# Rows of adjacency and x mapped by halves, and the first two outer products run in turn

## The chip, the cores and the metric

The kernel runs on one core of one Trainium2 chip. The metric is the device time of one execution in microseconds (us), the median of several runs.

## The reference

Sixteen graphs `x` of 1024 nodes with 128 features share one adjacency matrix `adj` (1024 x 1024), everything in fp32. Two layers follow each other, each closed by a residual sum and a layernorm over the features:

```python
def _L0_gnn_ref(x, adj, weight, bias):
    support = jnp.einsum('bnf,fo->bno', x, weight)
    output = jnp.einsum('nm,bmo->bno', adj, support)
    return output + bias
...
x = _layernorm(x + _L0_gnn_ref(x, adj, L0_gnn_weight, L0_gnn_bias), axis=-1)
x = _layernorm(x + _L1_gnn_ref(x, adj, adj, ...), axis=-1)
```

The second layer is a gated recurrent update of five steps. Each step multiplies every graph by `adj` and then applies gates with small weights (`w3`, `w4`, `w5`, `u3`, `u5`). The same product "adjacency times features" is thus made once in layer 0 and five times in layer 1.

## The kernel before

**The product.** The graphs are taken four at a time (`QUAD`), in four groups `q`. The product of `adj` with a group is made by Strassen's scheme in Winograd's form, two levels deep: an outer product of 2 x 2 blocks is seven block products, numbered 1 to 7, and each of those is again made of seven. The left factors of the outer level are `outer[1]` to `outer[7]`: 1 and 2 are the upper blocks of the transposed adjacency, 4 and 7 the lower ones, and 5, 6, 3 are the sums `s1`, `s2`, `s4`. `left[n]` holds the seven inner left factors of outer product `n`: some are quarters of `outer[n]`, the others sums in the tiles `e`. The right factors are pieces of the rows and sums of them, in `inner` and `tsum`.

**A chain.** `chain` (L358) runs the seven inner products for one or two outer products at once, in the order 1, 5, 6, 2, 7, 3, 4. One inner product of one outer product is two matmuls of 128x256 (L398). Results go to three PSUM banks: `pa` for 1 and 2, `pc` for 5 and 3, `pb` for 6, 7 and 4. After 1, ScalarE copies `pa` to `pb` (L382), so 6 has to wait for that copy, and 2 reuses `pa`. After 7 and 3, VectorE adds the bank to a result that was copied out before (L386, L387); after 5, 6, 2 and 4 ScalarE copies the bank out. `aggregate` (L417) calls the chains in the order 12 (outer products 1 and 2 together), 3, 67, 54. `hooks` are functions called ahead of a named inner product, which puts their instructions there in program order.

**The start.** The adjacency arrives as eight blocks `c` of 128 rows, 512 KB each, four into `agg` and four into `hid`; `x0` and `x1` stand between them in the queues of SP and ACT, `x2` and `x3` at the end (L127 to L133). Row `p`, chunk `c` of a graph is its row `8p + c`. `turn_adj` (L181) transposes a block on TensorE in two groups of four 128x128 pieces, one for each half `j` of the columns, into banks from a ring of three; VectorE copies out half 0 of the first four blocks (L193) and ScalarE everything else (L195), into `blk` (the tile `a`). Ahead of the transposes stand twelve products of the identity with itself (L200). Then come `inner_left_12`, the inner left sums for outer products 1 and 2 in four instructions 128x1024 wide (L168 to L171), the sums of the rows (L317 to L320), and the first chain, 12.

In the first group, the hooks of chain 12 bring in ahead of 5: `turn_rest`, the transposes of the last four blocks with the two halves of `s1` (L701); `added_sums`, which negates rows on ScalarE (L684) into `tsum[2]` and `tsum[0]` and issues from POOL a transfer that adds `x` to each (L685); and `added_left`, which negates `outer[7]` on ScalarE (L669) and adds `outer[1]` to it by two more transfers from POOL (L671). Ahead of 6 come `outer_left`, which makes `s2` (L705) and `s4` (L706), 128x2048 wide each, and the inner left sums of 3, and the row sums of 3. Ahead of 7 come `rest_sums` (L688, L689) and the inner left sums of 6 and 7. POOL then loads the next group's rows (L733).

**Order.** Each engine runs its instructions in the order of the built program. A scheduler makes that order; `keep_in_program_order` holds an instruction to its place in the source, and `issue_after` puts instructions behind another.

**After the first group**, chains, projections by `w0` with their layernorm, and later the gated steps follow each other on TensorE. Rows between steps go through DRAM (`turned`, `closing`, `hidden`); layer 0's result is kept in `saved`. Results leave through SP (L281), the last ones partly through ScalarE's queue (L296).

Of the kernel before, what the change touches and what calls it, by code (L numbers as in the profile page):

```python
# [20 lines left out]
def kernel(  # L21
# [76 lines left out]
            turns[0] = (i + 1) % 3  # L98
        return ps_m.tile([P, HALF], F32, tag=f"g{i}", name=name)

    def as_rows(b, src):
        return src[b].rearrange("(p c) d -> p c d", c=C)

    def chunked(t):
        return t.rearrange("p (c d) -> p c d", c=C)
# [4 lines left out]

    def load(q, dst, src_of, ks=range(QUAD)):
        for k in ks:
            nc.sync.dma_start(dst[:, k], src_of(q * QUAD + k))

    def x_rows(b):
        return x[b].rearrange("(p c) d -> p (c d)", c=C)

    def saved_rows(b):
        return saved[b]


    queues = (nc.sync, nc.scalar)

    adj_rows = adj.rearrange("(h p n c) m -> n h p c m", h=2, n=4, c=2)
    raws = [agg[:, c] if c < CH else hid[:, c - CH] for c in range(C)]

    for i, c in enumerate([*range(CH), "x0", "x1", *range(CH, C), "x2", "x3"]):  # L127
        queue = queues[i % 2 if i < 6 else 0]
        if isinstance(c, str):
            k = int(c[1])  # L130
            queue.dma_start(rows[:, k], x_rows(k))
        else:
            queue.dma_start(raws[c], adj_rows[c // 2, c % 2])  # L133
# [43 lines left out]
    def inner_left_12():  # L177
        a = [[blk[0][:, :, 2 * j : 2 * j + 2, ts(i, QT)] for j in range(2)] for i in range(2)]
        return left_sums(*a[0], *a[1], e12[:, :, 0], e12[:, :, 1], e12[:, :, 3], e12[:, :, 2])

    def turn_adj(c):  # L181
        cols = raws[c].rearrange("p (q k) -> p k q", k=C)
        i, at = divmod(c, CH)
        for j in range(2):
            pt = bank(f"pt_adj_{c}_{j}")
            pt3 = pt.rearrange("p (k q) -> p k q", k=CH)
            for k in range(CH):
                op = nc.tensor.transpose(pt3[:, k, :], cols[:, j * CH + k, :], ident)
                if c < CH:
                    tc.keep_in_program_order(op)  # L190
            dst = blk[i][:, j, :, ts(at, P)]
            if j == 0 and i == 0:
                nc.vector.tensor_copy(dst, pt3)  # L193
            else:
                nc.scalar.copy(dst, pt3)  # L195


    for t in (pb, *seeded):
# [1 line left out]
            nc.tensor.matmul(t[:, ts(k, P)], ident, ident, start=(k == 0), stop=True,  # L200
                             skip_group_check=True)
    for c in range(CH):
        turn_adj(c)
    last_left = inner_left_12()


    w0_sb = const.tile([P, D], F32, name="w0_sb")
# [41 lines left out]
    def layernorm(y, tag, store, now=False):  # L249
# [28 lines left out]
            )  # L278

        def put():  # L280
            nc.sync.dma_start(store, y)  # L281

        if now == "DVE":
            def step():
                for c in range(n):
                    pin(nc.vector.tensor_scalar(
                        y[:, c, :], y[:, c, :], shift[:, c : c + 1], rstd[:, c : c + 1],
                        ALU.add, ALU.mult,
                    ))
                put()  # L290
            return step
        elif now is True:

            for c in range(n):
                pin(apply(c))
            pin(nc.scalar.dma_start(store, y))  # L296
# [24 lines left out]

    def blocks_of(src, ns):

        if ns in ((1, 2), (3,)):
            v = src.rearrange("p b (h j x) -> p b h j x", h=2, j=2)
            if ns == (1, 2):
                return lambda j, k: v[:, k, :, j]
            return lambda j, k: v[:, 2 + k, 1:2, j]
        at = {(6, 7): slice(1, 3), (5, 4): slice(0, 4, 3)}[ns]
        return lambda j, k: tsum[:, at, k, ts(j, QT)]  # L330

    def sums_of(src, ns, pinned=False):
        t = inner[0 if ns in ((1, 2), (6, 7)) else 1]
# [24 lines left out]
    def chain(tag, src, turned, ns, results, hooks, order=(1, 5, 6, 2, 7, 3, 4)):  # L358

        xs = blocks_of(src, ns)
        t = inner[0 if ns in ((1, 2), (6, 7)) else 1]
# [53 lines left out]
    def aggregate(tag, src, hooks, turned=True):  # L417
# [8 lines left out]
            v = t.rearrange("p o (k i n) -> p o k i n", k=2, i=2)  # L426
            return lambda i, k: v[:, :, k, i]

        chain(f"12_{tag}", src, turned, (1, 2), into(first), hooks.get(12, {}))
        if turned:  # L430
            sums_of(src, (3,), True)
            outer = outer_sums(src, True, False, True)
# [27 lines left out]
    def project(q, k, y):  # L460

        b = q * QUAD + k
        y = chunked(y)
        for h in range(2):
            po = seeded[h]
            po3 = po.rearrange("p (k d) -> p k d", k=CH)
            with tc.high_priority():
                tc.keep_in_program_order(
                    nc.scalar.copy(po3, b0_bc[:, None, :].broadcast_to([P, CH, D]))
                )  # L470
            for c in range(CH):
# [6 lines left out]
        layernorm(y, f"0_{b}", chunked(saved[b]))  # L478

# [160 lines left out]
    def finish(q, k, y):  # L640
        for h in range(2):
            finish_half(q, k, h, chunked(y))

    def normalize(q, k, y, now=False):
        b = q * QUAD + k
        layernorm(chunked(y), f"1_{b}", as_rows(b, out), now)

    def normalize_part(q, k, cols, y, now):
        b = q * QUAD + k
        return layernorm(  # L650
            chunked(y)[:, cols], f"1_{b}_{cols.start}", as_rows(b, out)[:, cols], now
        )

    def call(f, *args):
        return lambda: f(*args)
# [2 lines left out]
    def projections(q):  # L658

        room = rooms[q % 2]  # L660
        ys = [ypad[0], ypad[1], room[:, 2], room[:, 3]]
        for k in (2, 3):
            nc.sync.dma_start(ys[k], x_rows(q * QUAD + k))
        return {a: [call(project, q, k, ys[k])] for k, a in enumerate((5, 2, 3, "end"))}

    def added_left():
# [7 lines left out]
    def added_sums():  # L674


        v = [
            x[2 * i : 2 * i + 2].rearrange("b (p c) d -> p b (c d)", c=C)[:, :, ts(j, HALF)]
            for j in range(2) for i in range(2)
        ]  # L680
        (lo, hi), ((lo0, hi0), (lo1, hi1)) = (rows[:, 0:2], rows[:, 2:4]), (v[:2], v[2:])
        put = tc.keep_in_program_order
        for i, negative, rest in ((2, hi[:, :, :HALF], hi1), (0, lo[:, :, :HALF], hi0)):
            put(nc.scalar.mul(tsum[:, i], negative, -1.0))  # L684
            put(nc.gpsimd.dma_start(tsum[:, i], rest, accum_op=ALU.add))  # L685
# [4 lines left out]

    rooms = [rows, hid]

    def turn_rest():
        for c in range(CH, C):
            turn_adj(c)
            if c % 2:
                outer_s1(c // 2 - 2)

    def outer_s1(at):
        cols = ts(at, QT)  # L700
        nc.vector.tensor_add(s1[:, :, cols], outer[7][:, :, cols], outer[4][:, :, cols])  # L701

    def outer_left():
        put = tc.keep_in_program_order
        nc.vector.tensor_sub(s2, s1, outer[1])  # L705
        put(nc.vector.tensor_sub(s4, outer[2], s2))  # L706
        inner_left(3)

    for q in range(NQ):
        room = rooms[q % 2]  # L710
        hooks = {}
        if q == 0:
            hooks[12] = {
                5: [turn_rest, added_sums, added_left],
                6: [outer_left, call(sums_of, rows, (3,))],
                7: [rest_sums, call(inner_left, 6), call(inner_left, 7)],
            }
            hooks[67] = {1: [call(inner_left, 5), call(inner_left, 4)]}
# [7 lines left out]
        def fetch(q=q):  # L726
            drain(99, 0)
            if q == 0:

                for dst, b in [(hid[:, k], QUAD + k) for k in range(QUAD)] + [  # L730
                    (ypad[k], k) for k in range(2)
                ]:
                    tc.keep_in_program_order(nc.gpsimd.dma_start(dst, x_rows(b)))  # L733
                load_layer1_weights()
                return
            for k in range(2):
                nc.sync.dma_start(ypad[k], x_rows(q * QUAD + k))
            if q + 1 < NQ:
                load(q + 1, rooms[(q + 1) % 2], x_rows)
            else:  # L740
# [11 lines left out]
        if q == 0:  # L752
            with tc.issue_after(last_left.ins):
                aggregate(f"x{q}", room, hooks, False)
        else:
            aggregate(f"x{q}", room, hooks, False)

# [3 lines left out]

    def close_load(q, k):
        fetch_rows(k, None, closing[k], ypad[0])
        tc.keep_in_program_order(nc.sync.dma_start(spare, saved_rows(q * QUAD + k)))

    def close(q, k):
        t = ypad[0].rearrange("p (n d c) -> p n c d", n=4, c=2)
        y = spare.rearrange("p (n c d) -> p n c d", n=4, c=2)  # L770
        tc.keep_in_program_order(nc.vector.tensor_add(y, y, t))
        strict[0] = True
        layernorm(chunked(spare), f"1_{q * QUAD + k}", as_rows(q * QUAD + k, out))
        strict[0], closed[0] = False, last_stats[0]

    def next_load(q, k):
        tc.keep_in_program_order(nc.sync.dma_start(spare, saved_rows(q * QUAD + k)))

    def next_turn(k):
        turn_hidden(k, spare, [ypad[1]])  # L780
# [175 lines left out]
```

## Time and profile before

| What | Value |
|---|---|
| median of 3 runs | 1771.18 us (1771.13 to 1771.88) |
| span of the profiled execution | 1769.3 us |
| what lies around the span, against the median | 1.9 us; the page gives no total of its own for the profiled execution |
| instructions | 19948 |
| HBM read and written | 93.98 MB and 65.01 MB |

The span runs from the first to the last instruction of the profiled execution; the runs are timed from outside, so a little more lies around it. "PE" is TensorE's matmuls, "PEld" its weight loads, "DVE" VectorE, "ACT" ScalarE, "POOL" GpSimd, "SP" SyncE; a "q" behind a name is that engine's queue of DMA issues. In a line of the timeline the first number is the start in us from the span's start, the second the duration, and the bracket at the end is the idle time before it and who ended it. The landing of a transfer is counted from its issue; the blocks of the adjacency took 4.0 to 10.3 us, the two transfers of L685 6.9 and 8.4 us, and the two of L671 9.0 and 10.6 us.

### The profile page before, as it was taken

What the parts mean: (1) busy time and instruction counts of PE and PEld (TensorE: products, weight loads), DVE (VectorE), ACT (ScalarE), POOL (GpSimd) and SP (SyncE); (2) the same over time, 40 slices, a digit from 0 to 9 for tenths busy, and PEclk for the clock granted to TensorE, in tenths of its full rate; (3) what the DMA queues carried; (4) which work ended last, traced back from release to release, by engine and by line L of the source; (5) the groups of instructions that cost most, each with busy time, mean ns of one, the idle gap of its engine ahead of it and who ended that gap; (6) DMA issues with size and microseconds to landing.
All of it is one profiled execution on the core that took longest, in us unless ns stands there. A gap on an engine that the chain in (4) does not pass through costs nothing.

```text
span 1769.3 us, 19948 instructions
## 1 busy us (share of the span) xinstructions
PE 1757.7 (99%) x6709; PEld 1264.5 (71%) x6709; DVE 1302.9 (74%) x2286; ACT 799.2 (45%) x1424; POOL 103.6 (6%) x152
## 2 busy tenths in 40 slices
PE   9999999999999999999999999999999999999997
PEld 8888885766758577685867758586675857668584
DVE  7977777676766857777777667777778577777778
ACT  4355555344352434435354442535445353443537
POOL 1202120000000000000000000000000000000004
PEclk9999999999999999999999999999999999999999
DMA  8144354141422505143351424324243241514232
GB/s 276 49 143 143 120 130 107 26 114 30 96 60 72 143 13 130 48 121 68 87 131 54 114 54 101 81 75 119 53 114 98 58 92 28 131 25 107 60 84 95
DMA packets 405332, 161.34 MB, mean 91 GB/s; under 512 B 388336, under 2 KB 389488, under 8 KB 405232
## 3 DMA queue, kind: packets, MB, share of 16 engines
q1 hardware_dynamic: 402960, 153.01, 34.1%
q0 software_dynamic: 1696, 5.24, 1.1%
q10 hardware_dynamic: 576, 1.84, 0.3%
q8 instruction: 53, 0.87, 0.2%
q14 instruction: 47, 0.39, 0.1%
HBM read 93.98 MB, written 65.01 MB: 90 GB/s over the span
## 4 chain that ended last, share of the span: by engine, by line
PE 98%; DMA 1%; DVE 0%; POOL 0%; ACT 0%; issue 0%; POOLq 0%; SPq 0%; DVEq 0%; ACTq 0%
PE pb L398 25%; PE pc L398 14%; PE pa L398 14%; PE pu L516 8%; PE ph L539 8%; PE ph L540 8%; PE pu L498 8%; PE seeded L531 8%; PE pc_x L398 3%; PE pa_x L398 3%; PE seeded L472 2%; DMA hid<-in_adj_dram 1%; DMA agg<-in_adj_dram 0%; PE pt L630 0%; PE pt_end L831 0%; POOL rstd L265 0%
## 5 line engine op out<-in xcount | busy, mean ns | idle before, releaser
L398 PE MATMUL pb<-e,inner 128*128 128x256 f32 x864 | 206.3, 379 | 0.2 <-ACT pb L382 0.2
L555 DVE TENSOR_TENSOR tsum<-tsum,hid 128x512 f32<-128x512 f32 x158 | 108.7, 688 | 106.4 <-ACT tsum L550 106.3
L550 ACT ACTIVATE tsum<-ph,bh 128x512 f32<-128x512 f32 x158 | 108.6, 687 | 164.3 <-PE ph L540 164.2
L398 PEld LDWEIGHTS pb<-e,inner 128*128 128x128 f32 x864 | 167.7, 194 | 19.5 <-ACT pb L382 0.9
L516 PE MATMUL pu<-agg,w_t 128*128 128x512 f32 x320 | 163.7, 593 | 0.0
L539 PE MATMUL ph<-agg,w_t 128*128 128x512 f32 x320 | 163.4, 592 | 0.0
L531 PE MATMUL seeded<-agg,w_t 128*128 128x512 f32 x320 | 163.4, 592 | 0.0
L540 PE MATMUL ph<-tsum,u_t 128*128 128x512 f32 x320 | 163.4, 592 | 0.0
L498 PE MATMUL pu<-hid,u_t 128*128 128x512 f32 x320 | 157.0, 592 | 0.0
L519 ACT ACTIVATE tsum<-pu,br 128x512 f32<-128x512 f32 x160 | 110.1, 688 | 85.5 <-PE pu L516 85.5
L398 PE MATMUL pb<-s,inner 128*128 128x256 f32 x576 | 148.4, 380 | 0.0
L398 PE MATMUL pb<-a,inner 128*128 128x256 f32 x576 | 143.9, 379 | 0.0
L526 DVE TENSOR_TENSOR tsum<-tsum,hid 128x512 f32<-128x512 f32 x160 | 110.2, 688 | 37.7 <-ACT tsum L519 37.7
L398 PE MATMUL pc<-e,inner 128*128 128x256 f32 x560 | 134.3, 379 | 0.0
L398 PEld LDWEIGHTS pb<-s,inner 128*128 128x128 f32 x576 | 110.5, 194 | 24.6 <-issue 10.2
L534 ACT ACTIVATE tsum<-seeded,bz 128x512 f32<-128x512 f32 x160 | 110.0, 688 | 29.3 <-PE seeded L531 29.3
L398 PEld LDWEIGHTS pb<-a,inner 128*128 128x128 f32 x576 | 111.9, 194 | 12.4
L398 PEld LDWEIGHTS pc<-e,inner 128*128 128x128 f32 x560 | 109.1, 195 | 12.7 <-issue 0.7
L540 PEld LDWEIGHTS ph<-tsum,u_t 128*128 128x128 f32 x320 | 60.8, 190 | 76.5 <-issue 59.1
L539 PEld LDWEIGHTS ph<-agg,w_t 128*128 128x128 f32 x320 | 60.6, 190 | 75.1 <-issue 74.4
L498 PEld LDWEIGHTS pu<-hid,u_t 128*128 128x128 f32 x320 | 60.8, 190 | 73.5 <-issue 72.2
L556 DVE TENSOR_TENSOR tsum<-tsum 128x512 f32<-128x512 f32 x158 | 109.1, 691 | 4.9
(192 smaller groups left out, 2856.3 us busy)
## 6 DMA issues: line engine op xcount, KB each, us to landing
turned<-ypad SPq DMA_DIRECT2D x48, 512.0 KB, 3.8
rows<-turned SPq DMA_DIRECT2D x192, 128.0 KB, 2.8
hvs<-saved SPq DMA_DIRECT2D x24, 512.0 KB, 4.1
rows<-saved SPq DMA_DIRECT2D x20, 512.0 KB, 3.8
hid<-hidden SPq DMA_DIRECT2D x64, 128.0 KB, 3.3
turned<-ypad SPq DMA_DIRECT2D x32, 256.0 KB, 2.9
rows<-turned SPq DMA_DIRECT2D x128, 64.0 KB, 2.1
hidden<-ypad SPq DMA_DIRECT2D x12, 512.0 KB, 4.1
```

The lines of the kernel that those rows point to most:

```text
L398: product = nc.tensor.matmul(bank_of[a][:, ts(o, QT)], chunk(a, o, c), left[n][a][:, c, :], start=(a in (1, 5) and o == 0 and c == 0), sto ...
L498: in_order(nc.tensor.matmul(pu, w_t["u3"], hid[:, k, ts(h, HALF)], start=True, stop=True, skip_group_check=True))
L516: in_order(nc.tensor.matmul(pu, w_t["w4"], agg[:, k, cols], start=False, stop=True, skip_group_check=True))
L519: pin(nc.scalar.activation(rh[:, cols], pu, AF.Sigmoid, bias=br))
L526: pin(nc.vector.tensor_mul(rh[:, cols], rh[:, cols], hid[:, k, cols]))
L531: in_order(nc.tensor.matmul(pz, w_t["w3"], agg[:, k, cols], start=False, stop=True, skip_group_check=True))
L534: pin(nc.scalar.activation(z_of[k % 2][:, cols], pz, AF.Sigmoid, bias=bz))
L539: in_order(nc.tensor.matmul(ph, w_t["w5"], agg[:, k, cols], start=True, stop=False))
L540: in_order(nc.tensor.matmul(ph, w_t["u5"], rh_of[k % 2][:, cols], start=False, stop=True))
L550: pin(nc.scalar.activation(hv, ph, AF.Tanh, bias=bh))
L555: pinned(nc.vector.tensor_sub(hv, hv, hid[:, k, cols]))
L556: pinned(nc.vector.tensor_mul(hv, hv, z_of[k % 2][:, cols]))
```

## The change

Row `p`, chunk `c` of a graph is now row `512h + 4p + c`, with `h` the half: a half of the chunks is a half of the graph's rows. The adjacency's rows follow the same rule, so that the left half of the columns of the first four blocks, with the first halves of `x0` and `x1`, holds all that outer product 1 needs. These come first, as 256 KB pieces on both queues; the second halves follow on SP, then the last four blocks, then `x2` and `x3`. ScalarE makes all copies of the transposes, and all transposes keep their program order.

In the first group, outer products 1 and 2 run as two chains one after the other. `inner_left_12` goes; `start_sums(n)` makes the inner left sums and the row sums of one outer product, in turn, 128x512 and 128x256 wide. The second halves of the first four blocks are transposed ahead of inner product 2 of chain 1, the last four blocks ahead of inner product 1 of chain 2. The other groups keep chain 12.

Stores to `out` are split in two where they hold all eight chunks; loads of `x` carry two runs of 2 KB for a partition instead of one of 4 KB.

```diff
-        return src[b].rearrange("(p c) d -> p c d", c=C)
+    def as_rows(b, src, h):
+        return src[b, ts(h, HALF)].rearrange("(p c) d -> p c d", c=CH)
...
-        return x[b].rearrange("(p c) d -> p (c d)", c=C)
+        return x[b].rearrange("(h p c) d -> p h (c d)", h=2, c=CH)
...
-    adj_rows = adj.rearrange("(h p n c) m -> n h p c m", h=2, n=4, c=2)
+    adj_rows = adj.rearrange("(i h p n c) m -> i n h p c m", i=2, h=2, n=2, c=2)
...
-    for i, c in enumerate([*range(CH), "x0", "x1", *range(CH, C), "x2", "x3"]):
...
+    for j in range(2):
+        for c in range(CH):
+            load_adj(queues[c % 2 if j == 0 else 0], c, ts(j, HALF))
+        for k in range(2):
+            load_x(queues[k if j == 0 else 0], k, j)
+    for c in range(CH, C):
+        load_adj(nc.sync, c)
+    for k in (2, 3):
+        nc.sync.dma_start(by_half(rows[:, k]), x_rows(k))
...
-            if j == 0 and i == 0:
-                nc.vector.tensor_copy(dst, pt3)
-            else:
-                nc.scalar.copy(dst, pt3)
+            nc.scalar.copy(blk[i][:, j, :, ts(at, P)], pt3)
...
-        turn_adj(c)
-    last_left = inner_left_12()
+        turn_adj(c, (0,))
...
-        chain(f"12_{tag}", src, turned, (1, 2), into(first), hooks.get(12, {}))
+        if 1 in hooks:
+            for n in (1, 2):
+                chain(f"{n}_{tag}", src, turned, (n,), into(first[:, n - 1 : n]), hooks[n])
+        else:
+            chain(f"12_{tag}", src, turned, (1, 2), into(first), hooks.get(12, {}))
...
+    def start_sums(n):
+
+        lt = left[n]
+        pairs = [
+            lambda: nc.vector.tensor_add(lt[5], quarter(n, 1, 0), lt[4]),
+            lambda: nc.vector.tensor_sub(lt[6], lt[5], lt[1]),
+            lambda: nc.vector.tensor_sub(lt[7], lt[1], quarter(n, 1, 0)),
+            lambda: nc.vector.tensor_sub(lt[3], lt[2], lt[6]),
+        ]
+        right = inner_sums(
+            blocks_of(rows, (n,)), [sums_for((n,))[:, i] for i in range(4)]
+        )
+        for f in pairs:
+            tc.keep_in_program_order(f())
+            tc.keep_in_program_order(next(right))
+
+    def turn_first_rest():
+        for c in range(CH):
+            turn_adj(c, (1,))
+        start_sums(2)
...
-        nc.vector.tensor_sub(s2, s1, outer[1])
+        put(nc.vector.tensor_sub(s2, s1, outer[1]))
+        sums_of(rows, (3,), True)
         put(nc.vector.tensor_sub(s4, outer[2], s2))
...
-            hooks[12] = {
-                5: [turn_rest, added_sums, added_left],
-                6: [outer_left, call(sums_of, rows, (3,))],
+            hooks[1] = {2: [turn_first_rest]}
+            hooks[2] = {
+                1: [turn_rest],
+                5: [added_sums],
+                6: [added_left, outer_left],
                 7: [rest_sums, call(inner_left, 6), call(inner_left, 7)],
             }
...
-            with tc.issue_after(last_left.ins):
-                sums_of(rows, (1, 2))
+            start_sums(1)
```

More of the change, by code (lines that the diff above doesn't have):

```diff
@@ L99, in bank @@
         return ps_m.tile([P, HALF], F32, tag=f"g{i}", name=name)
-    def as_rows(b, src):
-        return src[b].rearrange("(p c) d -> p c d", c=C)
+    def as_rows(b, src, h):
+        return src[b, ts(h, HALF)].rearrange("(p c) d -> p c d", c=CH)
     def chunked(t):
@@ L112, in load, with by_half, load_adj, load_x @@
         for k in ks:
-            nc.sync.dma_start(dst[:, k], src_of(q * QUAD + k))
+            nc.sync.dma_start(by_half(dst[:, k]), src_of(q * QUAD + k))
+    def by_half(t):
+        return t.rearrange("p (h y) -> p h y", h=2)
     def x_rows(b):
-        return x[b].rearrange("(p c) d -> p (c d)", c=C)
+        return x[b].rearrange("(h p c) d -> p h (c d)", h=2, c=CH)
     def saved_rows(b):
-        return saved[b]
+        return by_half(saved[b])
     queues = (nc.sync, nc.scalar)
-    adj_rows = adj.rearrange("(h p n c) m -> n h p c m", h=2, n=4, c=2)
+    adj_rows = adj.rearrange("(i h p n c) m -> i n h p c m", i=2, h=2, n=2, c=2)
     raws = [agg[:, c] if c < CH else hid[:, c - CH] for c in range(C)]
-    for i, c in enumerate([*range(CH), "x0", "x1", *range(CH, C), "x2", "x3"]):
[L128 to L131, printed above, removed]
-        else:
-            queue.dma_start(raws[c], adj_rows[c // 2, c % 2])
+    def load_adj(queue, c, cols=slice(None)):
+        queue.dma_start(raws[c][:, cols], adj_rows[c // 4, c // 2 % 2, c % 2][:, :, cols])
+    def load_x(queue, k, h):
+        queue.dma_start(rows[:, k, ts(h, HALF)], x_rows(k)[:, h])
+    for j in range(2):
[7 more added lines that the diff above has]
+        nc.sync.dma_start(by_half(rows[:, k]), x_rows(k))
     power = const.tile([P, C], F32, name="power")
@@ L175, in inner_left, with turn_adj @@
         left_sums(lt[1], lt[2], quarter(n, 1, 0), lt[4], lt[5], lt[6], lt[7], lt[3], *put)
[L177 to L182, printed above, removed]
+    def turn_adj(c, js=(0, 1)):
+        cols = raws[c].rearrange("p (j q k) -> p j k q", j=2, k=CH)
         i, at = divmod(c, CH)
-        for j in range(2):
+        for j in js:
             pt = bank(f"pt_adj_{c}_{j}")
@@ L187, in turn_adj @@
             for k in range(CH):
[L188 to L191, printed above, removed]
-            if j == 0 and i == 0:
-                nc.vector.tensor_copy(dst, pt3)
-            else:
-                nc.scalar.copy(dst, pt3)
+                tc.keep_in_program_order(
+                    nc.tensor.transpose(pt3[:, k, :], cols[:, j, k, :], ident)
+                )
+            nc.scalar.copy(blk[i][:, j, :, ts(at, P)], pt3)
     for t in (pb, *seeded):
@@ L280, in put @@
         def put():
-            nc.sync.dma_start(store, y)
+            for dst, of in store:
+                nc.sync.dma_start(dst, y[:, of])
         if now == "DVE":
@@ L295, in layernorm @@
                 pin(apply(c))
-            pin(nc.scalar.dma_start(store, y))
+            for dst, of in store:
+                pin(nc.scalar.dma_start(dst, y[:, of]))
         else:
@@ L322, in blocks_of @@
     def blocks_of(src, ns):
-        if ns in ((1, 2), (3,)):
+        if ns in ((1, 2), (3,), (1,), (2,)):
             v = src.rearrange("p b (h j x) -> p b h j x", h=2, j=2)
@@ L327, in blocks_of @@
                 return lambda j, k: v[:, k, :, j]
+            if ns in ((1,), (2,)):
+                return lambda j, k: v[:, k, ns[0] - 1 : ns[0], j]
             return lambda j, k: v[:, 2 + k, 1:2, j]
@@ L330, in blocks_of, with sums_for @@
         return lambda j, k: tsum[:, at, k, ts(j, QT)]
+    def sums_for(ns):
+        if ns in ((1,), (2,)):
+            return inner[0][:, :, ns[0] - 1 : ns[0]]
+        return inner[0 if ns in ((1, 2), (6, 7)) else 1]
     def sums_of(src, ns, pinned=False):
-        t = inner[0 if ns in ((1, 2), (6, 7)) else 1]
+        t = sums_for(ns)
         for op in inner_sums(blocks_of(src, ns), [t[:, i, : len(ns)] for i in range(4)]):
@@ L362, in chain @@
         xs = blocks_of(src, ns)
-        t = inner[0 if ns in ((1, 2), (6, 7)) else 1]
+        t = sums_for(ns)
         w = len(ns) * QT
@@ L477, in project @@
                 nc.vector.tensor_add(y[:, ts(h, CH), :], po3, y[:, ts(h, CH), :])
-        layernorm(y, f"0_{b}", chunked(saved[b]))
+        layernorm(y, f"0_{b}", [(chunked(saved[b]), slice(None))])
     strict = [False]
@@ L642, in finish, with both_halves @@
             finish_half(q, k, h, chunked(y))
+    def both_halves(b):
+        return [(as_rows(b, out, h), ts(h, CH)) for h in range(2)]
     def normalize(q, k, y, now=False):
         b = q * QUAD + k
-        layernorm(chunked(y), f"1_{b}", as_rows(b, out), now)
+        layernorm(chunked(y), f"1_{b}", both_halves(b), now)
     def normalize_part(q, k, cols, y, now):
         b = q * QUAD + k
-        return layernorm(
-            chunked(y)[:, cols], f"1_{b}_{cols.start}", as_rows(b, out)[:, cols], now
-        )
+        h, at = divmod(cols.start, CH)
+        part = chunked(y)[:, cols]
+        store = as_rows(b, out, h)[:, at : at + part.shape[1]]
+        return layernorm(part, f"1_{b}_{cols.start}", [(store, slice(None))], now)
     def call(f, *args):
@@ L662, in projections @@
         for k in (2, 3):
-            nc.sync.dma_start(ys[k], x_rows(q * QUAD + k))
+            nc.sync.dma_start(by_half(ys[k]), x_rows(q * QUAD + k))
         return {a: [call(project, q, k, ys[k])] for k, a in enumerate((5, 2, 3, "end"))}
@@ L677, in added_sums @@
         v = [
-            x[2 * i : 2 * i + 2].rearrange("b (p c) d -> p b (c d)", c=C)[:, :, ts(j, HALF)]
+            x[2 * i : 2 * i + 2, ts(j, HALF)].rearrange("b (p c) d -> p b (c d)", c=CH)
             for j in range(2) for i in range(2)
@@ L691 @@
     rooms = [rows, hid]
+    def start_sums(n):
[8 more added lines that the diff above has]
+            blocks_of(rows, (n,)), [sums_for((n,))[:, i] for i in range(4)]
+        )
+        for f in pairs:
[5 more added lines that the diff above has]
+        start_sums(2)
     def turn_rest():
@@ L700, in outer_s1 @@
         cols = ts(at, QT)
-        nc.vector.tensor_add(s1[:, :, cols], outer[7][:, :, cols], outer[4][:, :, cols])
+        tc.keep_in_program_order(
+            nc.vector.tensor_add(s1[:, :, cols], outer[7][:, :, cols], outer[4][:, :, cols])
+        )
     def outer_left():
         put = tc.keep_in_program_order
-        nc.vector.tensor_sub(s2, s1, outer[1])
+        put(nc.vector.tensor_sub(s2, s1, outer[1]))
+        sums_of(rows, (3,), True)
         put(nc.vector.tensor_sub(s4, outer[2], s2))
@@ L732, in fetch @@
                 ]:
-                    tc.keep_in_program_order(nc.gpsimd.dma_start(dst, x_rows(b)))
+                    tc.keep_in_program_order(nc.gpsimd.dma_start(by_half(dst), x_rows(b)))
                 load_layer1_weights()
@@ L736, in fetch @@
             for k in range(2):
-                nc.sync.dma_start(ypad[k], x_rows(q * QUAD + k))
+                nc.sync.dma_start(by_half(ypad[k]), x_rows(q * QUAD + k))
             if q + 1 < NQ:
@@ L751 @@
             hooks[54][4] = [turn_weights]
[L752 to L756, printed above, removed]
+        aggregate(f"x{q}", room, hooks, False)
     spare = hvs.rearrange("p h x -> p (h x)")
@@ L765, in close_load @@
         fetch_rows(k, None, closing[k], ypad[0])
-        tc.keep_in_program_order(nc.sync.dma_start(spare, saved_rows(q * QUAD + k)))
+        tc.keep_in_program_order(nc.sync.dma_start(by_half(spare), saved_rows(q * QUAD + k)))
     def close(q, k):
@@ L772, in close @@
         strict[0] = True
-        layernorm(chunked(spare), f"1_{q * QUAD + k}", as_rows(q * QUAD + k, out))
+        layernorm(chunked(spare), f"1_{q * QUAD + k}", both_halves(q * QUAD + k))
         strict[0], closed[0] = False, last_stats[0]
     def next_load(q, k):
-        tc.keep_in_program_order(nc.sync.dma_start(spare, saved_rows(q * QUAD + k)))
+        tc.keep_in_program_order(nc.sync.dma_start(by_half(spare), saved_rows(q * QUAD + k)))
     def next_turn(k):
```

## The prediction

> **What bounds the kernel now.** I read the busy shares first, then the chain of waits, then the waits of TensorE, then the first 62 us in order of time. From the page:
>
> ```profile
> PE 1757.7 (99%) x6709; PEld 1264.5 (71%) x6709; DVE 1302.9 (74%) x2286; ACT 799.2 (45%) x1424; POOL 103.6 (6%) x152
> ...
> PE 98%; DMA 1%; DVE 0%; POOL 0%; ACT 0%; issue 0%; POOLq 0%; SPq 0%; DVEq 0%; ACTq 0%
> ```
>
> TensorE (PE) is the bound: 98% of the chain is its own work, 1% the first loads. Asked for PE's waits between 62 and 1745 us, the trace names none. So what is lost or won at the start stands unchanged at the end, and only the start matters. Busy time by stretch there (PE, PEld, DVE, ACT, POOL, clock, DMA share, GB/s):
>
> ```profile
> 6.50:12.50 6.00, 6.00 (x42) 5.60 (x42) 3.68 (x5) 2.35 (x4) 0.00 (x0) 1.00 1.03 416
> 12.50:17.30 4.80, 4.41 (x35) 3.92 (x34) 4.80 (x6) 3.98 (x8) 0.00 (x0) 1.00 1.03 409
> 17.30:29.00 11.70, 11.70 (x56) 10.01 (x55) 11.70 (x15) 6.21 (x10) 7.12 (x9) 1.00 0.85 179
> 29.00:38.00 9.00, 8.09 (x37) 6.48 (x36) 8.73 (x15) 2.86 (x7) 0.53 (x1) 1.00 1.04 296
> 38.00:62.00 24.00, 24.00 (x112) 20.71 (x111) 23.99 (x37) 5.50 (x10) 0.00 (x0) 1.00 0.22 83
> ```
>
> From 12.5 to 62 VectorE (DVE) is as full as PE. The timeline, PE, its weight loads, DVE and ScalarE (ACT); start, duration:
>
> ```profile
> 3.01 3.53 PEld L200 LDWEIGHTS seeded<-ident 128*128 128x128 f32 x16
> ...
> 6.42 4.32 PEld L188 LDWEIGHTS pt_adj<-ident,agg 128*128 128x128 f32 x32
> ...
> 10.80 1.99 PE L398 MATMUL pa_x<-a,rows 128*128 128x256 f32 x8
> ...
> 15.02 0.97 PEld L188 LDWEIGHTS pt_adj<-ident,hid 128*128 128x128 f32 x8 [0.31 <-issue]
> ...
> 17.28 1.89 PE L398 MATMUL pc_x<-e,inner 128*128 128x256 f32 x8
> ...
> 18.90 2.00 ACT L684 ACTIVATE tsum<-rows 128x1024 f32<-128x1024 f32 x2 [0.79 <-DMA rows<-in_x_dram]
> ...
> 23.70 2.27 DVE L706 TENSOR_TENSOR s<-a,s 128x2048 f32<-128x2048 f32 x1
> ...
> 26.07 1.10 PE L398 MATMUL pa_x<-s,rows 128*128 128x256 f32 x4
> ...
> 36.99 1.13 PE L398 MATMUL pa_x<-s,tsum 128*128 128x256 f32 x4 [0.71 <-ACT pb L382]
> ```
>
> The first transposes start when the warm-up products (L200) leave PE at 6.5, not when their block lands (issued 0.73, landed 4.0 later). The 32 late transposes come in groups of eight 1.27 us apart: the pace of their loads, 512 KB each. And `s4` (L706) is ready at 25.97, when PE asks for it at 26.04.
>
> How much idle is there? PE's work from 6.4 to 62.8: 16 groups of four transposes at 0.54 (4.32/8) = 8.6; chains 12, 67 and 54 of 7 x 1.73 each (a product of two matmuls is 0.865) = 36.3; chain 3, 6.05; 3.0 of the next chain. Sum 54.0 of 56.4: **2.4 us idle**. The change leaves PE's work as it is, so 2.4 us (0.14%) is the most it can win.
>
> **What the Trainium skill says.** "Perfetto Trace Analysis", Identifying the Most-Contended Engine: matmul busy time overstates how near TensorE is to its peak. So I argue from waits; here PE is 99% busy, weight loads 71%. "VectorE: DVE Perf Modes", The TRN2 errata: an fp32 tensor_tensor takes (N+151)/0.96 ns, 424 for 256 and 2291 for 2048; the trace has 0.41 and 2.27, so it agrees. "DMA: Bandwidth & Descriptors", Anatomy of one DMA: 2.0 us and bytes over 436 GB/s, 3.2 us for 512 KB; the trace's accumulating transfers (L685, L671) took 6.9 to 10.6, so the trace decides. "TensorE: Matmul & The Clock Gate", Part 1: an idle window of about 3.4 us halves the clock; no wait of PE here after the start exceeds 0.7.
>
> **Durations used.** DVE's next instruction starts 0.34 after a 256-wide, 0.60 after a 512, 1.14 after a 1024, 2.20 after a 2048; ACT 0.26, 0.5, 0.95; a handover costs 0.04 to 0.07. Walking before's own order with these gives `s4` at 26.0 and chain 67's product 5 at 37.9; the trace has 25.97 and 37.96.
>
> **The change part by part**, in the order of the built program, on before's clock.
>
> 1. Loads by halves. x0's first half comes after 1.5 MB of stream instead of 3: about 7.2 for 10.8. PE still starts at 6.5. Sixteen transposes run to 8.6; all evictions are now ACT's, the last done at 9.4. Product 1 runs 8.6 to 9.5. Product 2 reuses `pa`, which ACT must first copy (0.37): idle 0.66. DVE's eight sums from 9.5 (0.60 and 0.34 in turn) let 5 and 6 run at 10.6 and 11.5 (0.09 idle). Four evictions of 0.6 leave DVE, but eight sums of 1.14 and 0.60 become sixteen of 0.60 and 0.34: about nothing.
> 2. The other 16 transposes from 12.4, the rest of product chain 1 to 17.7: idle 0.15, for DVE's add of 7 into the result.
> 3. The 32 late transposes, 17.7 to 21.9. Their loads landed by about 16.7, so the 0.5 lost to load pace goes.
> 4. Chain 2, seven products of 0.865, to 28.4: idle 0.46, mostly for product 4, whose bank DVE clears behind a 2048-wide sum.
> 5. **`s4`.** The last eviction ends at 22.7. DVE then needs 1.14 + 0.60 + 2.20 + six of 0.34 + 2.28: from 22.8 to 31.05. Before, the same stretch was covered by five products of 1.73 after the late transposes; now by chain 2 alone, 6.5 us. **Idle 2.7.**
> 6. Chain 3: product 2 waits for the copy of `pa` (0.66), 5 for its left sum (0.52, because the sum before it, L688, waits for the accumulate into `tsum`), 6 for 0.45.
> 7. **The accumulates.** The negation that begins them (L684, 18.9) now stands behind chain 2's first copy, at 23.3. Issues and landings move 4.4: the last `a` transfer from 34.7 to 39.1. DVE's first left sum of 7 waits for it, and queued behind on DVE stands chain 3's add of product 7, which frees `pb` for product 4. PE is ready at 38.8 and goes at 40.9: **idle 2.1.** Before, the same sum stood at 35.9, after both adds, and waited for nothing.
> 8. Chain 67: 0.9 for the copy of `pa`, as now. The next chain: 0.9, because the built order puts product 6 straight behind product 1.
>
> Sum 0.66 + 0.09 + 0.15 + 0.46 + 2.7 + 1.63 + 2.1 + 0.9 + 0.9 = 9.6 us idle, less the 2.4 of before: **+7.2 us**.
>
> Parts costed at nothing: 14 more stores on SP (about 0.33 us to issue each, 0.6 at most, so up to 8 us on that queue) and loads in 2 KB runs. SP mostly waits for DVE (668 us at L582 alone), and no PE wait after 62 us shows a fetch arriving late; if that slack were gone, rows fetched behind a store would be late by up to 0.6 eleven times, 6 us. POOL's six loads in two runs may take 1.4 to 1.7 to issue (as L685) for 0.6: ready about 46, first read after 56. The halves' rate is shown by no row: at 15% slower, taken as the far end, late transposes would still find their data within a microsecond; I take no loss, and exclude a gain because 420 GB/s holds already.
>
> The page gives a span of 1769.3 and no own total; the median run is 1771.18, so 1.9 lies around the span. The profiled execution stands for the median: 1771.2 + 7.2 = **1778.4 us**.
>
> **Rivals.** (a) The early start pays: the first loads are the chain's 1% of DMA, and all 2.4 us of idle go: 1768.8. For it: x0's half lands 3.6 earlier. Against: PE has work ahead of it in either order, and DVE is full. It decides where `s4` comes by 28.4 and the last accumulate by 37; I have 31.05 and 39.1. (b) The waits are smaller: both large ones go, since their landing is only shifted, not seen; 7.2 - 4.8 = +2.4, 1773.6, no measurable change. (c) The clock: 2.7 idle and two short waits near it halve PE's clock for a window or two of 3.4 us, +2 to +4: 1780.5 to 1782.5. (d) The change fails to do what it says: 2 KB runs or the two queues bring the half x0 at 10.8 as before; product 1 slips 2.2 and most is hidden behind DVE: +8 to +9, 1780.
>
> **Numbers.** Forecast as walked 0.68, (c) and (d) 0.17, (b) 0.12, (a) 0.03. Within 0.2% is 3.5 us, about what a measurement of this kernel can tell from no change: faster 0.03, same 0.12, slower 0.85. Range: half of each large wait gone gives +4.8, and with the short waits halved too about +3, so 1774.0; (c) gives 1782.5.
>
> **What would show it.** Right: a PE gap of 2 to 3 us ahead of the first `pa_x<-s,rows`, released by DVE's second 2048-wide `s`; one of about 2 ahead of chain 3's last product, with DVE waiting for `a<-a`; product 1 at 8.6; PE without waits after 85 us. Wrong: no DVE wait on a DMA, `s4` before chain 2 ends, or waits in the later steps.

## The result: 6.6 us slower, set by one transfer

The changed kernel takes 1778.09 us, the median of 5 runs (1777.05 to 1778.50); the kernel before took 1771.46 beside it. The ratio is 1.0037, 95% interval 1.0027 to 1.0048, so the change loses 6.6 us. The prediction was 1778.4. Its span is 1776.6 us, its own time 1778.5.

The page of the changed kernel: the busy shares have hardly moved, and the chain gives PE one per cent less.

```profile
PE 1759.9 (99%) x6709; PEld 1264.9 (71%) x6709; DVE 1301.1 (73%) x2292; ACT 801.6 (45%) x1433; POOL 101.8 (6%) x152
...
PE 97%; DVE 1%; DMA 1%; POOL 0%; SPq 0%; issue 0%; ACT 0%; POOLq 0%; DVEq 0%; ACTq 0%
```

PE's waits from 6 to 85 us (what, in total, how often, the longest); after 85 us there is a single one of 0.4. `L409` is the product of a chain (L398 before), `L393` the copy of `pa`, `L397` the add of product 7.

```profile
PE pa_x L409 <- issue: 2.5, 1, 2.5
PE pa_x L409 <- ACT pb L393: 1.7, 3, 0.7
PE pb L409 <- DVE agg L397: 1.3, 1, 1.3
PE pb L409 <- ACT pb L393: 0.7, 1, 0.7
```

The same windows as before, with the border at 38 moved to 45, where the stage now ends (PE, PEld, DVE, ACT, POOL, clock, DMA share, GB/s):

```profile
6.50:12.50 6.00, 5.55 (x31) 4.62 (x31) 2.75 (x6) 2.79 (x6) 0.00 (x0) 1.00 1.04 387
12.50:17.30 4.80, 4.80 (x30) 4.19 (x29) 2.89 (x7) 2.70 (x6) 0.00 (x0) 1.00 0.97 361
17.30:29.00 11.70, 11.11 (x64) 9.33 (x62) 10.32 (x18) 9.74 (x18) 4.47 (x5) 1.00 0.62 162
29.00:45.00 16.00, 11.48 (x43) 8.79 (x44) 13.16 (x19) 2.42 (x6) 4.39 (x6) 0.89 1.06 278
45.00:62.00 17.00, 17.00 (x79) 14.75 (x79) 16.90 (x25) 4.67 (x8) 0.00 (x0) 1.00 0.14 39
```

Most of the loss lies between 29 and 45: PE is busy for 11.48 of 16 us, where it was busy for 15.09 before, and its clock is 0.89, which takes up to 1.76 us more (16 times 0.11). The timeline, PE and then DVE, shows the two places (start, duration, and in brackets the idle time before it):

```profile
8.90 1.03 PE L409 MATMUL pa_x<-a,rows 128*128 128x256 f32 x4
...
17.88 4.03 PE L196 MATMUL pt_adj<-ident,hid 128*128 128x128 f32 x32
...
31.02 1.76 PE L409 MATMUL pa_x<-s,rows 128*128 128x256 f32 x4 [2.45 <-issue]
...
40.72 1.13 PE L409 MATMUL pb<-s,inner 128*128 128x256 f32 x4 [1.29 <-DVE agg L397]
```

```profile
28.64 2.28 DVE L749 TENSOR_TENSOR s<-a,s 128x2048 f32<-128x2048 f32 x1
...
39.03 0.69 DVE L179 TENSOR_TENSOR e<-a 128x512 f32<-128x512 f32 x1 [2.83 <-DMA a<-a]
39.64 0.68 DVE L180 TENSOR_TENSOR e<-e,s 128x512 f32<-128x512 f32 x1
40.24 0.42 DVE L397 TENSOR_TENSOR agg<-pb,agg 128x256 f32<-128x256 f32 x1
```

`s4` (L749) ends at 30.92, and chain 3 starts at 31.02 after 2.45 us of idle. The view names no releaser for that gap ("issue"); that it is `s4` is read from the times, which lie equally close in e8 below (29.32 and 29.42). Later DVE stands for 2.83 us at the first left sum of 7, until the transfer into `a` has landed; the add that frees `pb` is queued two instructions behind. But which of the two sets the end? The chain of waits, first 85 us (start, duration, what), answers that:

```profile
21.90 0.88 PE pa_x L409 x4
23.13 0.56 ACT tsum L703
23.69 0.40 issue
24.51 2.69 POOL tsum L704 x2
27.20 0.92 POOL a L690
28.14 10.80 DMA a<-a
39.13 0.51 issue
39.64 0.68 DVE e L180
40.72 1.13 PE pb L409 x4
```

The path leaves PE at chain 2's first product, goes through the negation that stands behind its copy, POOL's issues and the 10.80 us of the transfer, and comes back at 40.72. The gap ahead of chain 3 and the low clock after it lie beside this path, not on it.

### The profile page after: what moved, and what is told of

It reads as the page before. It is cut to its first block, busy times and chain, and to the rows that moved or that the text cites. A ratio compares the mean times of both kernels' runs of the same rounds, so it can differ in the third digit from the quotient of the medians.

```text
span 1776.6 us, 20008 instructions
## 1 busy us (share of the span) xinstructions
PE 1759.9 (99%) x6709; PEld 1264.9 (71%) x6709; DVE 1301.1 (73%) x2292; ACT 801.6 (45%) x1433; POOL 101.8 (6%) x152
## 4 chain that ended last, share of the span: by engine, by line
PE 97%; DVE 1%; DMA 1%; POOL 0%; SPq 0%; issue 0%; ACT 0%; POOLq 0%; DVEq 0%; ACTq 0%
PE pb L409 24%; PE pc L409 13%; PE pa L409 13%; PE ph L554 8%; PE ph L555 8%; PE pu L513 8%; PE seeded L546 8%; PE pu L531 8%; PE pa_x L409 3%; PE pc_x L409 3%; PE seeded L487 2%; DMA a<-a 1%; PE pt_adj L196 0%; DMA hvs<-saved 0%; SPq L608 0%; PE seeded L203 0%
## 5 line engine op out<-in xcount | busy, mean ns | idle before, releaser
L409 PE MATMUL pb<-e,inner 128*128 128x256 f32 x864 | 206.8, 379 | 0.7 <-ACT pb L393 0.7
L409 PEld LDWEIGHTS pb<-e,inner 128*128 128x128 f32 x864 | 167.6, 194 | 20.2 <-ACT pb L393 1.1
L409 PE MATMUL pb<-s,inner 128*128 128x256 f32 x576 | 148.6, 380 | 1.7 <-DVE agg L397 1.3
L409 PE MATMUL pb<-a,inner 128*128 128x256 f32 x576 | 144.3, 379 | 0.2 <-DVE first L397 0.2
L409 PE MATMUL pc<-e,inner 128*128 128x256 f32 x560 | 134.2, 379 | 0.0
L409 PEld LDWEIGHTS pb<-s,inner 128*128 128x128 f32 x576 | 110.2, 194 | 27.0 <-issue 10.4
L409 PEld LDWEIGHTS pb<-a,inner 128*128 128x128 f32 x576 | 111.8, 194 | 13.2 <-DVE first L397 0.9
L409 PEld LDWEIGHTS pc<-e,inner 128*128 128x128 f32 x560 | 109.1, 195 | 12.7 <-PE pu L513 0.7
```

What stands on the lines that cost most here:

```text
L409: product = nc.tensor.matmul(bank_of[a][:, ts(o, QT)], chunk(a, o, c), left[n][a][:, c, :], start=(a in (1, 5) and o == 0 and c == 0), sto ...
```

## The experiments

Each run stands beside runs of the kernel before on the same chip. "Over before" is the difference of the two medians.

| run | what | median us | over before | ratio (95%) |
|---|---|---|---|---|
| e1 | new mapping, old order | 1771.79 | +0.3 | 1.0002 (0.9993 to 1.0010) |
| e6 | half loads, one chain 12 | 1777.35 | +5.9 | 1.0034 (1.0021 to 1.0046) |
| e7 | e6, `s4` ahead of the adds | 1773.43 | +1.8 | 1.0010 (1.0003 to 1.0016) |
| e14 | e7, whole loads | 1771.46 | +0.1 | 1.0001 (0.9993 to 1.0009) |
| e3 | late transposes earlier | 1775.52 | +4.0 | 1.0024 (1.0015 to 1.0033) |
| e8 | `s4` straight behind `s2` | 1774.21 | +2.6 | 1.0017 (1.0010 to 1.0023) |
| e10 | three moves | 1774.75 | +3.2 | 1.0018 (1.0011 to 1.0025) |
| e2 | left sums of 7 later | 1776.41 | +4.9 | 1.0025 (1.0017 to 1.0033) |
| e25 | e2, 16 filler products | 1773.80 | +2.2 | 1.0013 (1.0006 to 1.0020) |
| e18 | e2, 8 filler products | 1773.20 | +2.1 | 1.0013 (1.0006 to 1.0019) |
| e5 | change, 16 filler products | 1778.08 | +6.7 | 1.0035 (1.0023 to 1.0047) |
| e17 | change, filler in both gaps | 1777.81 | +6.7 | 1.0039 (1.0026 to 1.0052) |

### Is it the mapping or the order? (e1)

The loads, copies, chain 12 and the hooks of before, on the new row mapping.

> The new mapping of rows with all that hangs on it (2 KB runs, stores split in two, column halves), but the instruction order of before at the start: whole loads in the old order, outer products 1 and 2 in one chain 12, VectorE sharing the copies of the transposes. Theory (the loss is the order of the first 62 us): the same as before within 0.2%, 1771.5 us, the first product of the chain after 67 at about 74.4 us as before, s4 ready at about 26. Rival (split stores, 2 KB runs or POOL's longer issues cost part of it): 1773.5 to 1778, with waits of PE after 85 us or loads that land late.

Measured: 1771.79, the same. PE waits once for `x` (0.5 us, at 11.26) and for nothing after 85 us. The row mapping, its 2 KB runs and the 14 more stores cost nothing that can be measured.

### Is it "in turn"? (e6, e7)

e6 keeps everything of the change but the two chains. All transposes of the first four blocks then stand ahead of chain 12:

```diff
...
-            hooks[1] = {2: [turn_first_rest]}
-            hooks[2] = {
-                1: [turn_rest],
-                5: [added_sums],
-                6: [added_left, outer_left],
+            hooks[12] = {
+                5: [turn_rest, added_sums, added_left],
+                6: [outer_left],
...
```

> The whole change (loads by halves, all copies of the transposes on ScalarE, pinned transposes) except that outer products 1 and 2 stay one chain of 1.73 us products with their sums 1024 wide. Theory (in turn is the cause, since chain 2 alone covers s4 with 6.5 us instead of five products of 1.73, and the accumulates start 4.4 us later): PE's gap ahead of chain 3 goes from 2.45 to under 0.5, the one ahead of its last product from 1.3 to under 0.3; 1771 to 1773.5 us, at most about 0.5 us lost because ScalarE alone ends the copies of the first transposes later. Rival (half loads or ScalarE's copies cause the loss): 1776 to 1778 us.

Measured: 1777.35. My theory fell: with one chain of 1.73 us products ahead, the kernel is nearly as slow. VectorE's timeline in e6 shows the larger part of the reason:

```profile
26.26 0.69 DVE L403 TENSOR_TENSOR first<-pb,first 128x512 f32<-128x512 f32 x1 [1.54 <-PE pb L415]
...
28.52 2.28 DVE L755 TENSOR_TENSOR s<-a,s 128x2048 f32<-128x2048 f32 x1
...
37.13 0.69 DVE L179 TENSOR_TENSOR e<-a 128x512 f32<-128x512 f32 x1 [1.04 <-DMA a<-a]
```

The pinned order of `outer_left` puts `s4` behind the adds of chain 12's products 7 and 3, so DVE waits 1.54 us for PE before it makes what PE needs next. Here too the clock drops (0.81 from 29 to 38 us in the profiled execution); but one of e6's five executions, at a mean clock of 0.999, took 1777.45 us all the same. PE also waits 1.0 and 0.9 us for blocks of the adjacency, which e14 takes up. e7 takes the pins of `s2` and of the row sums away, so that `s4` is built ahead of both adds:

```diff
-        put(nc.vector.tensor_sub(s2, s1, outer[1]))
-        sums_of(rows, (3,), True)
+        nc.vector.tensor_sub(s2, s1, outer[1])
         put(nc.vector.tensor_sub(s4, outer[2], s2))
...
-                6: [outer_left],
+                6: [outer_left, call(sums_of, rows, (3,))],
```

> The joint chain 12 with half loads and all copies of the transposes on ScalarE, as in the run with the joint chain, but VectorE makes s4 ahead of its adds of chain 12's products 7 and 3, as the kernel before does; in the run with the joint chain it stood behind both, idle for 1.54 us at the first. Theory (with enough matmul work in front, the place of s4 in VectorE's order decides): s4 starts at about 24.4 instead of 28.5, PE's gap of 1.3 ahead of chain 3 and the half clock after it go, 1772 to 1773.5 us. Rival (half loads and ScalarE's later copies cost the rest): 1775 to 1777 us.

Measured: 1773.43, by 4.0 us less than e6, with no gap ahead of chain 3. So the order on DVE makes most of the loss even where the chain is joint.

### What is left of e7? (e14)

e7 with whole blocks loaded, and transposed, in the old order; ScalarE still makes all the copies.

> The joint chain 12 with s4 first, as measured at 1773.4 us, with the loads as whole blocks in the order of before and the transposes block by block; ScalarE still makes all copies of the transposes. Theory (half loads in 2 KB pieces make PE wait for data, 0.91 us ahead of the second halves and 0.55 us ahead of the late blocks): these two waits go and the time is 1771.8 to 1772.3 us. Rival (ScalarE's late copies cost it, not the loads): 1773 to 1774 us, with the sums for chain 12 starting at about 12.3 instead of 11.4.

Measured: 1771.46, the same as before. In e7 PE waited for blocks (0.9 and 0.6 us); in e14 for one copy (0.7) and for `x` (0.6). The half loads cost the joint chain 1.7 us (1.8 over before in e7, 0.1 in e14), ScalarE's copies nothing that can be measured. The changed kernel doesn't pay that: no wait of PE there names a load, because the second halves are transposed only in the middle of chain 1.

### Moving the late transposes, and s4 (e3, e8, e10)

```diff
-            hooks[1] = {2: [turn_first_rest]}
+            hooks[1] = {2: [turn_first_rest], 7: [turn_rest]}
             hooks[2] = {
-                1: [turn_rest],
```

> The changed kernel with the transposes of the last four blocks, and with them the sums s1, moved ahead of chain 1's inner product 7 instead of chain 2's first product, so that s4's line of sums starts about two products earlier and stands before more matmul work. Theory (s4 waits for work on VectorE that starts with the last copy of a transpose): the gap ahead of chain 3 falls from 2.45 to about 1.0, and the half clock after it goes; with the accumulates earlier too, 1775 to 1776 us. Rival (VectorE is simply full up to then, so that order doesn't matter): the gap stays at 2.0 to 2.5, or as much idle appears in chains 1 and 2, 1777.5 to 1778.5 us.

Measured: 1775.52, as expected: the gap fell to 1.10. But PE waits of 0.88 appeared in chain 3 and in chain 67, and DVE now waits for both kinds of accumulating transfer (1.11 and 1.38 us). The accumulates did not come earlier: the negation still stands behind chain 2's first copy, and POOL issues the first transfer at 24.89 us (24.51 in the changed kernel).

```diff
         put(nc.vector.tensor_sub(s2, s1, outer[1]))
-        sums_of(rows, (3,), True)
         put(nc.vector.tensor_sub(s4, outer[2], s2))
+        sums_of(rows, (3,), True)
```

> The changed kernel, in turn, with s4 pinned straight behind s2, so that the four row sums of outer product 3 (4 x 0.34) no longer stand ahead of it; by the built order the left sum of 7 that waits for the accumulating transfer then also stands behind chain 3's adds. Theory: s4 ready 1.3 to 1.4 earlier, gap ahead of chain 3 1.1 instead of 2.45, no wait for the accumulates, no half clock: 1773.5 to 1775 us. Rival (the row sums are late instead and chain 3's product 5 waits for them, or the clock halves all the same): 1776 to 1778 us.

Measured: 1774.21. The exchange of two lines wins back 3.9 us, though it shortens the gap by only 1.0 (to 1.45). In the built order the left sum of 7 also comes later here, behind both adds of chain 3, and finds its transfer landed:

```profile
38.62 0.68 DVE L179 TENSOR_TENSOR e<-a 128x512 f32<-128x512 f32 x1
```

e10 makes the moves of e3, e8 and e2 together.

> The changed kernel, in turn, with three moves: the transposes of the last four blocks ahead of chain 1's product 7, s4 straight behind s2, and the left sums of 7 behind chain 3. Walk: s2 ends at 24.4, s4 at 27.1, before chain 2 ends at about 28; the accumulates are waited for by nothing; PE's idle time is then the copies of pa (0.45 to 0.71 three times) and some tenths. Theory: no gap of over 1 us, clock 0.998 to 0.999, 1770.5 to 1772.5 us, the same as before. Rival (running in turn costs more by itself, since chain 1 and 2 each wait for their own copy and VectorE is full): 1774 us or more.

Measured: 1774.75, the rival's time. No gap is over 1 us and the clock is full, but PE now waits for the transfer itself, which my walk had ruled out, and for ScalarE's copies (three of PE's waits):

```profile
PE pa_x L409 <- ACT pb L393: 1.2, 2, 0.7
PE pa_x L409 <- DMA a<-a: 0.8, 1, 0.8
PE pa_x L409 <- ACT rows L396: 0.7, 1, 0.7
```

### The sum that waits for the transfer, and the clock (e2, e25, e18)

e2 moves the left sums of 7 behind chain 3:

```diff
-                7: [rest_sums, call(inner_left, 6), call(inner_left, 7)],
+                7: [rest_sums, call(inner_left, 6)],
             }
+            hooks[3] = {"end": [call(inner_left, 7)]}
```

> The changed kernel with the inner left sums of outer product 7 moved behind the end of chain 3, so that VectorE's add of chain 3's product 7 no longer stands behind a sum that waits for the accumulating transfer. Theory: PE's wait of 1.3 us ahead of chain 3's last product falls to about 0 to 0.1 and the time by 1.2 to 1.4 to 1776.8 us, if chain 67 is then not held by the same sums. Rival (the half clock after the 2.45 us gap was hidden behind that wait or the transfer is waited for elsewhere): the wait turns up again later, chain 67 starts where it did, and the time stays at 1778.1 within 0.5.

Measured: a median of 1776.41, but from 1772.96 to 1777.83. The two quickest of 13 executions (1772.96, 1773.86) ran at a mean clock of 0.999, two (1774.62, 1774.82) at 0.998, the other nine (1775.80 and up) at 0.997. The median lies near the 1776.8 that I expected, but not for my reason, as e18 will show. The profiled one was the quickest: still the gap of 2.45, but neither the wait for the transfer nor a low clock. e25 and e18 test that reading: they add products of the identity in the gap, behind chain 2.

```diff
+    def keep_busy():
+        for t in (*seeded, *seeded):
+            for k in range(CH):
+                tc.keep_in_program_order(nc.tensor.matmul(
+                    t[:, ts(k, P)], ident, ident, start=(k == 0), stop=True,
+                    skip_group_check=True,
+                ))
...
+                "end": [keep_busy],
```

> The kernel with the left sums of 7 moved later, and in addition sixteen products of the identity with itself (about 2.2 us, their result is not used) on TensorE at the end of chain 2, where it idles 2.45 us for s4. Theory (executions of the kernel without the filler spread from 1773.0 at a mean clock of 0.999 to 1777.8 at 0.997, so an idle gap of 2.45 us halves the clock in most of them, at 1 to 5 us each): all executions at a clock of 0.998 to 0.999 and 1773 to 1774 us. Rival (the spread has another cause, such as the landing of the transfers): median and spread stay at about 1776.4 and 5 us.

Measured: 1773.80, 21 executions from 1773.06 to 1774.91, all at 0.998 or 0.999. The filler was mis-sized: it ran from 27.99 to 31.56, 3.57 us, and held chain 3 back. e18 takes half of it (`for t in seeded`):

> The kernel with the left sums of 7 moved later and a filler of half the size, eight identity products (1.8 us, results not used), which ends before s4 is ready; sixteen took 3.57 us and held chain 3 back by about 1.1. Theory: clock full in all executions, 1772.6 to 1773.1 us, as the quickest execution without filler (1773.0). Rival (the 0.6 us of idle left in the gap still halves the clock in some, or the size of the filler was no loss): 1773.6 to 1775 us with a spread over 2 us.

Measured: 1773.20, from 1772.55 to 1774.18, a little above what I expected; the other half of the filler had cost 0.6 by medians, 0.1 against before. The half clock after the gap is thus real: e2 loses 2.8 us to it (4.9 less 2.1 over before). So the move of e2 wins 4.5 us once the clock is kept (6.6 less 2.1), and 1.7 without that.

### Does the changed kernel pay for the clock? (e5, e17)

e5 is the changed kernel with e25's filler, nothing moved.

> The changed kernel with nothing moved, and sixteen products of the identity with itself (about 2.2 us, result not used) on TensorE in its 2.45 us gap at the end of chain 2. Theory (the half clock of about 3.5 us after the gap costs 1.7 us of TensorE's speed, but in the changed kernel this is hidden, because VectorE's sum that waits for the accumulating transfer sets chain 3's last product at about 40.7 in either case): PE's wait there grows from 1.3 to 2.5 to 3.1 and the time stays at 1777.5 to 1778.5 us. Rival (the half clock is paid in full): 1775.5 to 1776.5 us with the wait still at 1.3.

Measured: 1778.08, no gain, as the theory had it. Filling the first gap only makes the second one longer, and in the profiled execution the clock falls there instead: 0.81 over 38 to 47 us.

```profile
40.28 1.57 PE L409 MATMUL pb<-s,inner 128*128 128x256 f32 x4 [2.39 <-DVE agg L397]
```

Its six executions split by the clock: three at 0.998 or 0.999 took 1776.21 to 1777.48, three at 0.997 took 1778.68 to 1779.18. So e17 puts eight filler products into both gaps (`hooks[3] = {4: [keep_busy]}` besides).

> The changed kernel with nothing moved, with eight products of the identity with itself (1.8 us by the 3.57 us that sixteen took, results not used) in each of its two gaps on TensorE: at the end of chain 2, and ahead of chain 3's last product. Theory (the executions of the changed kernel show clocks of 0.996 to 0.998; without a half clock the same waits give what the two quick executions with one filler gave): all executions at a clock of 0.998 to 0.999 and 1776.0 to 1776.9 us, so the clock is 1.2 to 2.1 of the change's 6.6 us. Rival (the half clock is hidden behind the wait for the transfer): the clock is full all the same, and the time stays at 1777.6 to 1778.2.

Measured: 1777.81, at 0.998 and 0.999 in all five executions. My theory fell, the rival holds: with a full clock the kernel is as slow. DVE still waits for the transfer in e17:

```profile
38.35 0.69 DVE L179 TENSOR_TENSOR e<-a 128x512 f32<-128x512 f32 x1 [2.61 <-DMA a<-a]
```

e17 and e18 have the same clock and differ in the place of the left sums of 7 and in e17's second filler: 6.7 against 2.1 over before. **DVE's wait for the transfer, with the sums that it holds back, is worth about 4.6 us, everything else in the change 2.1.** The trace of e17 shows what the 4.6 is made of. Its second filler takes 1.95 us where PE would otherwise stand idle; PE then waits 0.97 us for the add that frees `pb`, and once more for the first right sum of chain 67, which DVE reaches only behind the sums that were held back:

```profile
44.07 1.97 PE L409 MATMUL pc_x<-e,inner 128*128 128x256 f32 x8 [1.61 <-DVE inner L321]
```

e18 has none of the three, some 4.5 us in all. Two limits remain. The changed kernel has another order on PE there and not this wait of 1.61: from the moment DVE goes on to the product `pc_x<-e,hid`, e17 takes 43.14 us and the changed kernel 42.53, so up to 0.6 of the 4.6 may be e17's own, and the clock may cost the changed kernel as much. And no run brings the transfer itself earlier with the sums left in place; the wait and the place of the sums were only moved together.

## Why the prediction was right

The total was off by 0.3 us. The product `pc_x<-e,hid` of the chain that follows, which started at 74.35 before, starts at 81.56: 7.2 later, as the walk had it. Step by step:

- **Steps 1 to 4** held. Product 1 at 8.6 (measured 8.90), the wait for the copy of `pa` 0.66 (0.45), the other transposes from 12.4 (12.73), the late ones 17.7 to 21.9 (17.88 to 21.74), chain 2 to 28.4 (28.57), but 0.15 of listed idle in it instead of 0.46.
- **Step 5** held: `s4` ready at 31.05 (30.92), idle 2.7 (2.45). What I gave as its reason, that chain 2 alone is too short a cover, is only half of it: e6 has the long cover and still a gap of 1.30, because DVE makes adds ahead of `s4`. In the changed kernel itself both count: with the row sums behind `s4` (e8) a gap of 1.45 is left.
- **Step 6** was over-sized: 1.63 for chain 3's short waits, where only 0.50 is listed. The half clock, up to 1.76 us, which the forecast had left to rival (c), took its place, so that product 4 was asked for at 39.4 instead of 38.8. That the total came within 0.3 us is in part luck.
- **Step 7** held in time and mechanism, and was wrong in weight. The negation was put at 23.3 (23.13), but chain 2's copy ahead of it is only 0.6 of the delay: ScalarE copies the late transposes, which now stand behind chain 1, until 22.56. The transfer's landing was put at 39.1 (DVE goes on at 39.03), the product at 40.9 (40.72), the idle time at 2.1 (1.29, as PE came late). I added this to `s4`'s 2.7. In truth the two are not a sum: the transfer's path sets 40.7 whatever happens before, and the gap, the first copies and the clock vanish in the wait. A walk in order of time gets the right end from both views, but a reader of the sum would have mended `s4` first. Filling that gap won nothing in e5; only where DVE's order changed as well (e3, e8) did an earlier `s4` pay.
- **Step 8**: 0.71 twice for 0.9 twice. e2's trace has neither; e8 and e10, where DVE doesn't stand for the transfer, have one of 0.71 each, as the kernel before has. So they depend on the built order, and which part of it brings them is not shown.
- **Costed at nothing**: stores, 2 KB runs and POOL's issues, rightly (e1). Half loads too, since the second halves aren't asked for at once (e14 shows what they cost where they are).
- **The rivals.** (a) and (d) failed: product 1 did start 1.9 us earlier than before (8.90 for 10.80), and no gain followed. Sixteen transposes, which take 2.1 us, had only moved from ahead of it to behind it, so TensorE had done no more work by then. (c) came true in the records and not in the time: the clock halved, but e17, with a full clock, is no quicker (6.7 over before, where the change has 6.6). (b) was wrong for this kernel, and is roughly e18.

No version here beats the kernel before: e14 and e1 equal it, and every kernel here that runs 1 and 2 in turn lies 2.1 us or more above it. With at most 2.4 us of idle in the old start, there was little to win.

## What to carry to other kernels

Don't add up idle times that follow each other before you have asked which path sets the last of them: where a later instruction waits for a transfer that the gap doesn't delay, an earlier gap of the same engine is free up to that wait, and filling it won nothing here (e5). When a block of work is started earlier or split, follow what it pushes back on the other queues: here the late transposes and chain 2's first copy came ahead of a negation on ScalarE, and a transfer of 10.8 us moved with it by 4 us. And put the instruction that waits for a transfer behind those that free banks for TensorE. That was worth 1.7 us alone, since the half clock then took part of it back, and about 4.6 with the clock kept full; two exchanged lines, which moved that instruction too, won back 3.9.

## What I had not expected of the hardware

- **The clock.** A single idle gap of 2.45 us was followed by half clock in most executions. In e2, 9 of 13 have a mean clock of 0.997; in e18, where 0.67 us of the gap was left, all 21 have 0.998 or 0.999, as the kernel before has. "Half" is read from the trace: behind the gap the first four matmuls of the changed kernel take 1.76 us, while four take 0.88 at 21.90. In e6's profiled execution it took no more than gaps of 1.30 and 0.50 us, 1.1 us of work apart; in e8's a gap of 1.45 was not followed by it. In the changed kernel PE's clock was 0.89 over 16 us, which is some 3.5 us at half. The prediction relied on the Trainium skill, "TensorE: Matmul & The Clock Gate", Part 1, for an idle window of about 3.4 us; here 2.45 us were enough, so the measurement decides. The same part says that the window runs freely and doesn't reset when a kernel starts; that one kernel's executions differ fits this, but no run here shows the window itself.
- **The start.** The identity products ahead of the transposes are the same in every kernel here, and yet the first transpose starts anywhere from 5.52 us (e18) to 6.63 us (before and the change) in the profiled executions. So a shift of up to 1.1 us between two traces need not come from an edit. Why it varies is not shown.
- **Half loads.** From 6.5 to 12.5 us the stream ran at 387 GB/s in the changed kernel and at 366 to 386 in the other profiles with half loads; with whole blocks it ran at 416 (before), 406 (e1) and 400 (e14). The size of a piece (256 KB for 512) and the length of its runs (2 KB for 4) were not varied apart.
- **Identity products.** Sixteen of 128x128 in fp32 took 3.57 us, 0.22 each; a transpose of the same size took 0.13 (32 in 4.03). The trace has two matmul records for each such product and one for each transpose, so a filler has to be priced by its own row: my 2.2 us for sixteen was about the price of as many transposes.
